# Setup of a graph-attention kernel: the q term in four column groups, the first mask counts in a step of their own, and the row flags read back half a batch later

## The chip, the core and the metric

The kernel runs on one core of a Trainium2 chip. The metric is the device time of one execution in microseconds, as the median of several. One execution was taken with the hardware profiler. Its views name the engines PE (matmul), PEld (weight load, beside PE), DVE (VectorE), ACT (ScalarE), POOL (GpSimd) and SP (the engine that issues most DMAs; "SPq" is its queue of issues).

## The reference, cut to what matters

```python
B, N, F = 16, 512, 512          # x; q is 16 x 512; the mask is 16 x 512 x 512 x 11 int32
H, dh, NONGT = 16, 32, 20       # heads, their width, keys per node
row_zero = x.sum(-1) == 0
q_exp = where(row_zero, 0, q[:, None, :])
self_feat = concat([x, q_exp]) @ W_self.T + b_self
output = self_feat
for d in range(2):              # the mask, and its transpose
    A = (mask if d == 0 else mask^T)[:, :, :20, :]
    cond, vb = A.sum(-1), A @ w_bias + b_bias
    qh = (self_feat @ Wq[d].T + bq[d]).reshape(B, N, H, dh)
    kh = (self_feat[:, :20] @ Wk[d].T + bk[d]).reshape(B, 20, H, dh)
    aff = where(cond > 0, einsum(qh, kh) / sqrt(dh), -9e15) + vb
    w = softmax(aff)
    output += einsum(einsum(w, self_feat[:, :20]), Wout[d]) + bout[d]
return x + relu(output)
```

All arithmetic is in float32.

## The kernel before, in words

**Setup, first part (lines 360 to 469).** The kernel first makes the self features of the 20 key nodes of all 16 batches (320 columns). SP issues the loads in the order of lines 379 to 400: the key columns `xkv` and the weights `ws_v` in three pieces, q as `q_sb`, the q half of the weights as `ws_q` (1 MB), then the key weights `wk`, `wq_sb`, the first x and mask tiles, and so on. PE multiplies `ws_v` with `xkv` into four PSUM banks `ps_kv` (L409). The q term is a product of its own: 16 matmuls `ps_q` (L424), each with a 128x128 block of `ws_q` as the weights and the 16 columns of `q_sb` as the moving operand. DVE copies the result to `qw` (L429). A matmul with a matrix of ones (`ps_nzk`, L434) sums x over the features, and DVE turns the sums into flags `nzk` (L435). DVE and POOL multiply flags and q term (`qp`, L442), DVE adds `ps_kv` (`kvn`, L446), ACT adds the bias (`kvT`, L449). PE then makes keys per direction and block (`ps_k`, L456), and ACT writes them to `khT` (L460).

**Setup, second part (lines 481 to 607).** The query weights are folded into the keys. Of 64 pieces PE makes three at a time, a burst: `keys(runs)` has four 32-row matmuls a piece (L534), two go to one pair of PSUM banks and two to a second pair. ACT copies the first pair to a staging tile `st` (L549), DVE the second (L551), and the next burst may overwrite a pair only after its copy. SP writes the tiles to DRAM (`g_d`, L554 to L558). There are 22 bursts, numbered n. Between two bursts the code puts other work, listed in `other`: the biases, the row flags of batches 0 and 1 (`row_flags`), the scores of the bias (`ps_c`, L487, four column groups of 32; their results go out through eight small DMAs that POOL issues, L494), the first self features (`ps_sf`, L186) and the values (`ps_v`, L507, whose results POOL writes out as `vw_d`, L517).

Three pieces of the main loop's work for batch 0 are put there by number: after burst 6 `mask_mul(0, 0)` and `mask_count(0, 0)`, after burst 8 `mask_add(0, 0)`, `load_cq(0)` and `row_sums(1)`, after burst 18 `full_add(0, 0)`. A mask half (256 nodes) passes through three steps. `mask_mul`: ACT casts the 880 integers to float (L207), POOL multiplies them with the bias weights (L208). `mask_count`: DVE counts the entries (L213) and turns the counts into 0 or -9e15 (L214). `mask_add`: DVE reduces the products (`lb`, L220), adds (L222), and ACT spreads the result (`both`, L227). `row_sums(1)` is three additions on POOL (`rx`, L163 and L165).

The order on each engine follows the program, but the scheduler moves some instructions of the main loop up: the count of mask half (0, 1) stands on DVE beside that of (0, 0), and the cast and product of (0, 1) stand on ACT and POOL within the bursts. The product tile `prod` has one buffer, so the second cast waits until the first product has been reduced (L220).

**Main loop.** For each of 16 batches there are four tiles nt of 128 nodes. A tile has the matmuls of the next self features (`ps_sf`, L186) and the scores (`ps_s`, L246), softmax on DVE, ACT and POOL, and once per batch the attention matmuls of the batch before (`ps_o`, L311) and the output. PE, DVE, ACT and POOL each keep an order of their own; SP issues in program order and waits at each issue for what that transfer needs. From batch 2 on the row flags take a way through DRAM: at nt 3 of batch b `row_mask(b + 2)` makes them on DVE and writes 2 KB to `nz_d` (L154), and right behind it `load_nz(b + 2)` reads them back to all partitions (L158). They are first used by `self_copy` (L199) at nt 3 of batch b + 1.

## Time and profile before

| | us |
|---|---|
| median of 3 runs (lowest, highest) | 644.77 (643.81, 644.95) |
| the profiled execution's own time | 644.1 |
| its span, first to last instruction | 642.2 |
| PE busy | 623.5 |
| DVE busy | 525.1 |
| POOL busy | 335.7 |
| ACT busy | 217.0 |

The profiled execution took 644.1 us in all, 0.7 us less than the median, of which 642.2 us lie between its first and last instruction. Busy times are sums over an engine's instructions. A wait "[2.93 <-DVE st L551]" behind a row means that the engine stood idle for 2.93 us before it, and that the copy at line 551 on DVE ended the wait. PEclk is the share of the full TensorE clock that was granted in a stretch.

### The profile page before, as it was taken

What the parts mean: (1) busy time and instruction counts of PE and PEld (TensorE: products, weight loads), DVE (VectorE), ACT (ScalarE), POOL (GpSimd) and SP (SyncE); (2) the same over time, 40 slices, a digit from 0 to 9 for tenths busy, and PEclk for the clock granted to TensorE, in tenths of its full rate; (3) what the DMA queues carried; (4) which work ended last, traced back from release to release, by engine and by line L of the source; (5) the groups of instructions that cost most, each with busy time, mean ns of one, the idle gap of its engine ahead of it and who ended that gap; (6) DMA issues with size and microseconds to landing.
All of it is one profiled execution on the core that took longest, in us unless ns stands there. A gap on an engine that the chain in (4) does not pass through costs nothing.

```text
span 642.2 us, 16385 instructions
## 1 busy us (share of the span) xinstructions
PE 623.5 (97%) x6830; PEld 373.7 (58%) x6830; DVE 525.1 (82%) x815; ACT 217.0 (34%) x479; POOL 335.7 (52%) x252
## 2 busy tenths in 40 slices
PE   8998999999999999999999999999999999999992
PEld 7654446655566565656565656565656565656552
DVE  0558554989898989899898989898989898989896
ACT  0334431415242424333242424252525151523232
POOL 1307121534738282837474747465565657474754
PEclk9898999999999999999999999999999999999997
DMA  8987899676546465656474646575746565644112
GB/s 289 397 331 248 344 370 342 174 230 213 199 154 222 156 213 157 204 165 222 147 234 146 224 153 231 154 242 155 242 154 227 169 211 186 209 122 145 66 67 100
DMA packets 89921, 131.87 MB, mean 205 GB/s; under 512 B 9240, under 2 KB 59960, under 8 KB 87800
## 3 DMA queue, kind: packets, MB, share of 16 engines
q1 hardware_dynamic: 89176, 129.47, 60.3%
q0 software_dynamic: 672, 1.36, 0.8%
q8 instruction: 54, 0.88, 0.6%
q14 instruction: 19, 0.16, 0.1%
HBM read 90.89 MB, written 39.92 MB: 204 GB/s over the span
## 4 chain that ended last, share of the span: by engine, by line
PE 84%; DVE 2%; ACT 1%; issue 0%; DVEq 0%; ACTq 0%
PE ps_s L246 43%; PE ps_sf L186 33%; PE ps_o L311 6%; PE ps_v L507 1%; ACT o L729 0%; PE ps_nz L169 0%; DVE s L284 0%; DVE mx L275 0%; DVE o L725 0%; DVE s L276 0%; PE ps_g(3, 0, 1, 1, 2)0_687 L534 0%; PE ps_g(3, 3, 0, 0, 2)0_764 L534 0%; PE ps_g(3, 2, 0, 1, 2)0_738 L534 0%; PE ps_g(3, 1, 1, 0, 2)0_710 L534 0%; DVE ps_s L273 0%
## 5 line engine op out<-in xcount | busy, mean ns | idle before, releaser
L246 PE MATMUL ps_s<-g,sf 128*64 128x320 f32 x2048 | 286.9, 433 | 0.0
L186 PE MATMUL ps_sf<-x,ws_v 128*64 128x256 f32 (+1 forms) x2048 | 221.4, 371 | 0.0
L246 PEld LDWEIGHTS ps_s<-g,sf 128*64 128x64 f32 x2048 | 145.8, 137 | 125.4 <-issue 6.2
L186 PEld LDWEIGHTS ps_sf<-x,ws_v 128*64 128x64 f32 x2048 | 146.7, 137 | 71.9 <-issue 1.7
L293 POOL TENSOR_TENSOR s<-s,sm 128x640 f32<-128x640 f32 x63 | 80.1, 1271 | 146.8 <-DVE sm L292 145.5
L266 ACT ACTIVATE s<-s 128x640 f32<-128x640 f32 x63 | 46.5, 738 | 239.8 <-DVE s L261 239.8
L236 POOL TENSOR_TENSOR full<-cq,both 128x640 f32<-128x640 f32 x64 | 99.1, 1548 | 27.0 <-ACT both L227 23.5
L208 POOL TENSOR_TENSOR prod<-prod,wb_sb 128x880 f32<-128x880 f32 x32 | 61.3, 1916 | 57.3 <-ACT prod L207 57.3
L257 DVE TENSOR_TENSOR ps_s<-ps_s,full 128x640 f32<-128x640 f32 x63 | 52.3, 830 | 42.5 <-PE ps_s L246 42.4
L333 POOL TENSOR_TENSOR o<-o,x 128x512 f32<-128x512 f32 x60 | 75.2, 1274 | 0.0
L227 ACT COPY both<-add 64x80 f32<-64x80 f32 x128 | 32.8, 256 | 76.1 <-DVE add L222 75.0
L291 DVE TENSOR_REDUCE sm<-s 128x32 f32<-128x640 f32 x63 | 51.7, 820 | 6.0 <-ACT s L266 0.9
L199 DVE SCALAR_TENSOR_TENSOR sf<-nz,qw,ps_sf 128x236 f32<-128x236 f32 (+1 forms) x128 | 52.6, 458 | 3.0 <-PE ps_sf L186 3.0
L259 DVE TENSOR_REDUCE mx<-ps_s 128x32 f32<-128x640 f32 x63 | 51.9, 824 | 2.2
L261 DVE TENSOR_TENSOR s<-ps_s,mx 128x640 f32<-128x640 f32 x63 | 51.9, 824 | 2.2
L300 DVE STREAM_TRANSPOSE wt<-s 128x640 f32<-128x640 f32 x63 | 52.5, 834 | 0.0
L311 PE MATMUL ps_o<-wt,vd 32*32 32x256 f32 (+2 forms) x2176 | 46.3, 374 | 6.3 <-issue 4.0
L330 ACT ACTIVATE o<-o,bo 128x512 f32<-128x512 f32 x60 | 40.0, 714 | 27.4 <-DVE o L324 25.0
L311 PEld LDWEIGHTS ps_o<-wt,vd 32*32 32x32 f32 x2176 | 31.0, 103 | 22.1 <-issue 14.6
L324 DVE TENSOR_TENSOR o<-ps_o,sf 128x512 f32<-128x512 f32 x60 | 36.3, 667 | 0.0
L213 DVE TENSOR_REDUCE cond<-adj 128x80 f32<-128x880 int32 x32 | 33.1, 1036 | 1.8 <-DMA adj<-in_adj 1.8
L149 ACT ACTIVATE xn<-xn 128x512 f32<-128x512 f32 x56 | 34.3, 614 | 0.0
(199 smaller groups left out, 440.5 us busy)
## 6 DMA issues: line engine op xcount, KB each, us to landing
g<-g_d SPq DMA_DIRECT2D x15, 1280.0 KB, 6.3
g_d<-st SPq DMA_DIRECT2D x16, 1120.0 KB, 5.5
x<-in_xT SPq DMA_DIRECT2D x16, 1024.0 KB, 9.3
out_T<-o SPq DMA_DIRECT2D x61, 256.0 KB, 2.0
xn<-in_xn SPq DMA_DIRECT2D x28, 512.0 KB, 6.6
adj<-in_adj SPq DMA_DIRECT2D x32, 440.0 KB, 8.6
vd<-bd_d SPq DMA_DIRECT2D x64, 128.0 KB, 2.6
nz<-nz_d SPq DMA_DIRECT2D x14, 256.0 KB, 4.0
```

The costliest lines, as they stand in the source:

```text
L186: nc.tensor.matmul(held[0][bass.ts(a, R), i * N // 2 : i * N // 2 + hi - lo], ws_v[:, k, bass.ds((2 * f + i) * P + a * R, R)], xs[b][:, k, ...
L199: nc.vector.scalar_tensor_tensor(sfs[b][:, 2 * f + i, lo:hi], nzs[b][:, lo:hi], qw[:, 2 * f + i, b : b + 1], ps[:, i * N // 2 : i * N // 2 ...
L208: nc.gpsimd.tensor_mul(p, p, wb_sb.unsqueeze(1).to_broadcast([P, 2 * S, L]))
L236: nc.gpsimd.tensor_add(f, cqs[b].unsqueeze(1).to_broadcast(shape), adds[b, nt // 2][:, nt % 2].unsqueeze(2).to_broadcast(shape),)
L246: nc.tensor.matmul(ps[bass.ts(a, R), g, : W // 2], sfs[b][:, k, bass.ds(nt * P + g * R, R)], keys[:, k, a], start=(k == 0), stop=(k == C - 1),
L257: nc.vector.tensor_add(pw, pw, fulls.pop((b, nt)).rearrange("p g h m -> p g (h m)"))
L259: nc.vector.tensor_reduce(mx, p4, AX.X, ALU.max)
L261: nc.vector.tensor_sub(s, p4, mx.unsqueeze(3).to_broadcast(full))
L293: nc.gpsimd.tensor_mul(s, s, sm.unsqueeze(3).to_broadcast(full))
L300: nc.vector.transpose(wts[b][:, nt], s.rearrange("p a h m -> p (a h m)"))
L311: nc.tensor.matmul(banks[q][bass.ts(e, DH)].rearrange("p (t n) -> p t n", n=32), vds[b][r, e, i, q // 2 * 2 + n], wt[r, :, bass.ts(j, 32)] ...
L333: nc.gpsimd.tensor_add(o[:, c], o[:, c], xs[b][:, c])
```

## The change: what it does

**The q term.** `q_sb` becomes four blocks of 32 columns, of which 16 hold q and 16 are set to zero by DVE. Instead of 16 matmuls there are four, one for each block of 128 inputs: the weights are the 32 columns of `q_sb`, the moving operand is a 512-column row of `ws_q`, and each writes a column group of its own of one PSUM bank. ACT copies this bank to `q4`. Four further matmuls with a 0/1 matrix `sel` (128x16) sum the four groups and turn the result to the layout of before. POOL makes `sel` at the start with a memset and four `affine_select` instructions. The four last matmuls and the copy to `qw` come between the products of column blocks 2 and 3. The sums for the flags go to the second bank of the same PSUM tile.

**The first masks.** `mask_count(0, 0)` stays after burst 6, `mask_mul(0, 0)` moves to after burst 7, `mask_add(0, 0)` and `load_cq(0)` to after burst 9, `row_sums(1)` to after burst 11. A mask tile is no longer removed from its table when it is counted.

**The row flags.** `load_nz(b + 1)` is issued at nt 1 of batch b behind `load_cq(b + 1)`, half a batch after the write.

```diff
-        a = adjs.pop((b, h))
+        a = adjs[b, h]
...
-        q_sb = sp.tile([P, C, B], F32, name="q_sb")
+        q_sb = sp.tile([P, C, DH], F32, name="q_sb")
+        sel = sp.tile([P, B], F32, name="sel")
...
             nc.vector.memset(ones, 1.0)
+            nc.vector.memset(q_sb[:, :, B:], 0.0)
             nc.vector.memset(bqbd, 0.0)
             nc.gpsimd.memset(zero, 0.0)
+            nc.gpsimd.memset(sel, 0.0)
+            for k in range(C):
+                nc.gpsimd.affine_select(
+                    out=sel, in_=sel, pattern=[[-1, B]], compare_op=ALU.not_equal, fill=1.0,
+                    base=-k * DH, channel_multiplier=1,
+                )
...
-            rows(q_sb, qT)
+            rows(q_sb[:, :, :B], qT)
...
-            ps = ps_s.tile([P, 2, 512], F32, tag="s", name="ps_q")
-            for fc in range(C):
-                for i in range(C):
-                    nc.tensor.matmul(
-                        ps[:, fc % 2, fc // 2 * B : (fc // 2 + 1) * B],
-                        ws_q[:, i, bass.ts(fc, P)], q_sb[:, i],
-                        start=(i == 0), stop=(i == C - 1),
-                    )
-            nc.vector.tensor_copy(qw..., ps...)
-            ps = ps_s.tile([P, 2, 512], F32, tag="s", name="ps_nzk")
-            nc.tensor.matmul(ps[:, 0, :BM], ones, rsk, start=True, stop=True)
-            nc.vector.tensor_scalar(nzk, ps[:, 0, :BM], 0.0, None, ALU.not_equal)
+            ps = ps_s.tile([P, 2, 512], F32, tag="s", name="ps_q4")
+            for k in range(C):
+                nc.tensor.matmul(ps[bass.ts(k, DH), 0], q_sb[:, k], ws_q[:, k], start=True, stop=True)
+            q4 = sk.tile([P, F], F32, name="q4")
+            nc.scalar.copy(q4, ps[:, 0])
+            nc.tensor.matmul(ps[:, 1, :BM], ones, rsk, start=True, stop=True)
+            nc.vector.tensor_scalar(nzk, ps[:, 1, :BM], 0.0, None, ALU.not_equal)
             for fc in range(2, C):
                 for k in range(2, C):
                     kv_terms(fc, k)
+                if fc == 2:
+                    ps = ps_s.tile([P, 2, 512], F32, tag="s", name="ps_q")
+                    for c in range(C):
+                        nc.tensor.matmul(
+                            ps[:, c % 2, c // 2 * B : (c // 2 + 1) * B], q4[:, bass.ts(c, P)], sel,
+                            start=True, stop=True,
+                        )
+                    nc.vector.tensor_copy(qw..., ps...)
...
                 if n == 6:
+                    mask_count(0, 0)
+                if n == 7:
                     mask_mul(0, 0)
-                    mask_count(0, 0)
-                if n == 8:
+                if n == 9:
                     mask_add(0, 0)
                     load_cq(0)
+                if n == 11:
                     row_sums(1)
...
                         load_cq(b + 1)
+                        if b > 0:
+                            load_nz(b + 1)
...
-                    if nt == 3:
-                        load_nz(b + 2)
```

More of the change, by code (lines that the diff above doesn't have):

```diff
@@ L419, in gat_kernel @@
                     kv_terms(fc, k)
-            ps = ps_s.tile([P, 2, 512], F32, tag="s", name="ps_q")
-            for fc in range(C):
-                for i in range(C):
-                    nc.tensor.matmul(
-                        ps[:, fc % 2, fc // 2 * B : (fc // 2 + 1) * B],
-                        ws_q[:, i, bass.ts(fc, P)], q_sb[:, i],
-                        start=(i == 0), stop=(i == C - 1),
-                    )
-            nc.vector.tensor_copy(
-                qw.rearrange("p (i a) b -> p a i b", a=2),
-                ps[:, :, : 2 * B].rearrange("p a (i b) -> p a i b", b=B),
-            )
-            ps = ps_s.tile([P, 2, 512], F32, tag="s", name="ps_nzk")
-            nc.tensor.matmul(ps[:, 0, :BM], ones, rsk, start=True, stop=True)
-            nc.vector.tensor_scalar(nzk, ps[:, 0, :BM], 0.0, None, ALU.not_equal)
+            ps = ps_s.tile([P, 2, 512], F32, tag="s", name="ps_q4")
[5 more added lines that the diff above has]
+            nc.vector.tensor_scalar(nzk, ps[:, 1, :BM], 0.0, None, ALU.not_equal)
             for fc in range(2, C):
@@ L438, in gat_kernel @@
                     kv_terms(fc, k)
+                if fc == 2:
[5 more added lines that the diff above has]
+                        )
+                    nc.vector.tensor_copy(
+                        qw.rearrange("p (i a) b -> p a i b", a=2),
+                        ps[:, :, : 2 * B].rearrange("p a (i b) -> p a i b", b=B),
+                    )
             for fc in range(C):
```

## The prediction

> **What bounds the kernel now.** I read the chain that ended last first.

> ```profile
> span 642.2 us, 16385 instructions
> ...
> PE 623.5 (97%) x6830; PEld 373.7 (58%) x6830; DVE 525.1 (82%) x815; ACT 217.0 (34%) x479; POOL 335.7 (52%) x252
> ...
> PE 84%; DVE 2%; ACT 1%; issue 0%; DVEq 0%; ACTq 0%
> ```

> 84% of the chain is matmul work. The parts of the change that lie in the main loop therefore gain only where PE stands idle. The waits of PE, longest first, say where:

> ```profile
> PE ps_o L311 <- issue: 4.0, 2, 2.8
> PE ps_g(1, 2, 0, 0, 2)1_489 L534 <- DVE st L551: 2.9, 1, 2.9
> PE ps_o L311 <- DVE wt L285: 2.3, 1, 2.3
> PE ps_warm L370 <- DVE ones L365: 1.1, 1, 1.1
> PE ps_q L424 <- DMA ws_q<-in_wsT: 0.9, 1, 0.9
> ```

> Of the first row 2.8 us and all of the third lie in the tail, which is not touched; 1.19 us lie in the first attention, at 146. The second row is the large one. The timeline around it:

> ```profile
> 54.26 3.77 DVE L214 TENSOR_SCALAR cond<-cond 128x80 f32<-128x80 f32 x2
> 54.83 1.92 POOL L208 TENSOR_TENSOR prod<-prod,wb_sb 128x880 f32<-128x880 f32 x1
> 55.57 0.81 PE L534 MATMUL ps_g(1, 2, 0, 0, 2)0_488<-khT,wq_sb 32*128 32x320 f32 x4
> 56.70 1.27 POOL L163 TENSOR_TENSOR rx<-x 128x512 f32<-128x512 f32 x1
> 57.96 1.21 DVE L551 TENSOR_SCALAR st<-ps_g(1, 1, 0, 1, 2)1_462 128x320 f32<-128x320 f32 x2
> ...
> 59.31 0.54 PE L534 MATMUL ps_g(1, 2, 0, 0, 2)1_489<-khT,wq_sb 32*128 32x320 f32 x2 [2.93 <-DVE st L551]
> ```

> Two instructions on 80 numbers hold DVE for 3.77 us. Their row alone shows 2.562 and 1.291 us; the shortest of all 32 of this line takes 0.201. The first ends at 56.82 and the second at 58.03, each as an instruction of POOL ends. The copy behind them is late, and PE waits for the bank. The clock then falls (columns: stretch, length, busy time with counts of PE, PEld, DVE, ACT, POOL, granted clock, DMA share, GB/s):

> ```profile
> 13.10:16.50 3.40, 3.40 (x31) 3.40 (x32) 0.00 (x0) 1.28 (x1) 0.00 (x0) 1.00 1.05 397
> 16.60:19.90 3.30, 3.30 (x8) 2.22 (x8) 1.85 (x5) 0.21 (x1) 1.20 (x2) 0.50 1.06 401
> ...
> 56.40:59.30 2.90, 0.00 (x0) 0.02 (x1) 2.90 (x5) 0.00 (x0) 2.82 (x3) 1.00 0.67 255
> 59.30:60.90 1.60, 1.59 (x14) 1.10 (x15) 1.02 (x3) 0.66 (x2) 1.27 (x2) 1.00 0.19 58
> 61.00:64.20 3.20, 3.20 (x16) 1.18 (x18) 1.98 (x4) 1.73 (x5) 0.48 (x1) 0.50 1.00 371
> ```

> It is at 0.50 after the stall, and also from 16.6 to 19.9, behind 3.4 us of the 16-column matmuls `ps_q`.

> **The change part by part. Masks.** Between the end of the `ps_sf` matmuls at 55.57 and the end of burst 11 (the start of `ps_v` at 70.38) PE takes 14.8 us. Later bursts without a wait take 1.03 (72.29 to 73.32), a group of `ps_v` 1.91 with four records and 1.18 with two: four bursts and their groups would take 9.1, so 5.7 us are lost: 3.7 in the stalled burst, 1.6 in the two slow rows at half clock, 0.4 later.

> In the changed order `mask_mul(0, 0)` comes behind burst 7's copies on ACT. The cast (0.94) then starts when these end, POOL's product 55.9 instead of 54.83. In times of before: the two counts end at 54.35. POOL issues the eight `cq_d` transfers until 54.81. If these issues hold DVE as the product does, the L214 pair ends at 55.2 (two of 0.20 behind 54.81), 0.7 before the product; if they do not, at 54.8. The copy L551 (1.21) ends at 56.4 instead of 59.17. PE wants that bank some 0.4 after 55.57. Burst 6, whose second pair came 0.71 late, took 1.72; here it comes 0.9 late, so I take 1.95 for burst 8, a loss of 0.9.

> A new wait stands in place of the old one. `lb` (L220, 1.06) and L222 (0.30 here) now follow the copies of burst 9 on DVE, and on ACT the cast of mask half (0, 1), which waits for `lb`, and the four `both` copies stand before the copy of burst 10. In times of before: burst 8 ends at 57.5, `ps_v` 59.4, burst 9 60.5, copies on DVE to 61.8, `lb` to 62.9; cast 0.93, `both` 1.05, copy 1.03 on ACT to 65.9. PE comes to burst 11 at 57.5 + 1.91 + 1.03 + 1.18 + 1.36 (a burst with a slightly late pair, as at 83.31) + 1.91 = 64.9. It waits 1.0 and ends the burst at 66.9 instead of 70.4. **Masks: -3.5** (to -5.4 if neither wait shows, to 0 if the pair is still held).

> `row_sums(1)` takes 3.9 us of POOL behind `vw_d`'s first issue; its reader at 93.39 has over 20 us of cover, and the `vw_d` issues behind it are wanted at 116.5. `load_cq(0)` moves past three SP issues (about 1.6 us); its reader is at 94.57. Both cost 0; without that cover they would cost at most 3.9 and 1.6.

> **q.** Removed: 16 matmuls, 3.77 us. Added: four with 512 columns. The nearest row is `ps_c`, also four column groups: eight matmuls of 320 columns take 1.28 us, which serial at 2 x 0.267 each would be 4.3. Scaled to four of 512: 1.0 (serial 3.4). From 13.05, when `ws_q` lands as before, they end at 14.05. The matmul for the flags now writes the same PSUM tile that ACT copies to `q4`, and in the changed program it waits for ACT: copy of 128x512 about 0.7 (ACT rows of that width: 0.61 to 0.71), so PE is idle to 14.9; queued behind it are all PE's next products. Flags 0.55, column block 2 1.07, four `sel` matmuls 0.92 (eight records of 0.115 as in `ps_q`), to 17.45. `qw` ends at 17.8, and DVE's row `qp` starts there instead of 18.64; `nzk` is out of its way. The 3.8 us from it to the last `kvT` stay, so PE's `ps_k` gains 0.8. Key weights are there: SP's issue at 23.93 ended a wait for `wq_sb`, needed at 25.35 after the shift. The table load on ACT waits for nothing now and moves to the start.

> Against that stands the clock. **Row:** a stretch with 1.6 us of work in some 3.4 (the idle stretch and the one behind it) was followed by half clock; the first attention, with 1.19 idle in 3.4, was not (1.00 after it). So the limit lies between 47% and 65%. [...] By the row, the 3.4 us from 16.5 hold about 1.7 of streaming (column block 3 1.07, 0.5 of `ps_k`, 0.1 of `sel`), 50%, near the row that was throttled. Half clock over `ps_k` eats the 0.8, and 0.8 more if it falls where PE doesn't wait for `kvT` anyway. The row decides on the masks. For q I take **-0.4**, halfway between warm and cold, since 50% lies inside the open interval; ends -0.8 and +0.8.

> On POOL, `sel`'s memset and four `affine_select` precede the sums `rsk`. No row shows them; memsets are 0.1 to 0.2, a 128x320 addition 0.86. POOL is idle from 0.93 to 4.88, and `rsk` (ends 9.08) is wanted at 14.9: 9.8 us of cover. I take 0. Bounds: nothing, and what passes 9.8. DVE's memset of `q_sb` (nearest, 0.27) is done long before the load.

> **Row flags.** `load_nz` leaves the place where SP waited for the 2 KB write (7.5 us in its first three). Behind it stood stores and `xn` loads, for which no engine on the chain waits. At its new place it adds one issue of 0.33 behind `cq`, with nothing to wait for. In batch 2 `cq` is issued by 172.0, the first use is at 193.9 (127.23 plus two batches of 33.35): 22 us for a landing of 3.7 to 4.9. **0.** Bounds: 1.2 gained if the first attention's wait went, 1.0 lost if the earlier `xn` load slowed the mask tile that DVE waits for at 136.75 (the 2 KB write behind that tile landed with it, so transfers do not overtake, and I take nothing).

> A second cost has no cover to spare: with the stall gone, bursts follow at 2.94 us throughout, where DMA share was 0.94. A late last `g_d` would move what follows; up to 1, in the range.

> **Sum.** -3.5 - 0.4 = -3.9 on the profiled execution, whose own time is 644.1 (span 642.2 and 1.9 around): 640.2. The median lies 0.67 above it, so **640.9**.

> **The rivals.**
> - More goes (0.16): clock warm, the ACT wait hidden, perhaps the first attention's wait gone too. -3.5 - 1.0 - 0.8 - (0 to 1.2): 638.3 to 639.5, say 638.6. For it: 0.5 to 1 us decide. Against: ACT's order has no gap there.
> - Part of it is given back through DMA or cold q (0.10): 642.3.
> - The change doesn't do what it says (0.08): L214 is still held, because the pair isn't through before POOL's product starts. It is held to that product's end, PE waits nearly 3 us again, and only about 0.8 remains: 644.0. It decides where DVE is 0.7 later than worked out.
> - Slower (0.04): `affine_select` is long. It delays `rsk`, and PE's queue behind the flags. It decides over 9.8 + 3.9 = 13.7 us for the four, 3.4 each; at 5 each, 10.2 late, 651.1. Against: 16 columns, and all other POOL rows.
> - The forecast itself: 0.62, 639.9 to 641.9.

> **How the numbers follow.** 0.2%, 1.3 us, is about what a measurement of this kernel can tell from no change. Faster: 0.62 + 0.16 + 0.10 = 0.88; same 0.08; slower 0.04. The range 638.5 to 643.0 leaves out the last two cases and about half of the first rival, 0.2 in all.

> **What would show it.** L214 near 0.2 to 0.8 each and before the product; PE's 2.9 us wait gone, and a wait of about 1 at burst 11 on ACT's copy; no half clock near 61; four `ps_q4` in 1.0 and PE idle 0.8 behind them; `ps_k` 0.4 to 0.8 earlier; from burst 11 on everything 3.9 earlier. It is wrong if PE still waits for L551 near 56, if `rsk` ends after 14, or if the main loop gains or loses by batch.

## The result, and the profile after

| | before | after |
|---|---|---|
| median of 4 runs, us (lowest, highest) | 644.29 (642.81, 644.95) | 638.66 (638.31, 639.12) |
| the profiled execution's own time | 644.1 | 639.12 |
| its span | 642.2 | 637.0 |

The medians are 5.6 us apart, where 3.9 less had been forecast. The ratio is 0.989 (95% interval 0.9861 to 0.9919); the two medians alone make 0.991. The direction is right, the size is not: the forecast ratio, 640.9 / 644.77 = 0.994, lies outside the interval. The median is only just within the forecast range of 638.5 to 643.0, and the ratio, taken of the 644.77 that the forecast started from, makes 637.7, which is below it.

PE's busy time fell from 623.5 to 618.3, although no matmul of the main loop is gone:

```profile
PE 618.3 (97%) x6814; PEld 368.8 (58%) x6814; DVE 521.6 (82%) x816; ACT 217.5 (34%) x480; POOL 336.6 (53%) x257
```

Of PE's waits, the 2.9 us on L551's copy is gone. A shorter one on ACT's copy at burst 11 stands in its place, and in q's part there are new ones, on the copy of q and on `kvT`:

```profile
PE ps_k L469 <- ACT kvT L462: 1.1, 2, 0.8
...
PE ps_g(2, 0, 0, 1, 2)0_570 L547 <- ACT st L562: 0.9, 1, 0.9
PE ps_q L435 <- ACT q L434: 0.8, 1, 0.8
```

The timeline of the same place. The first three rows answer to the prediction's third block, the others are the chain that the prediction foresaw (`lb`, cast, `both`, copy, burst 11):

```profile
48.23 5.14 POOL L507 DMA_DIRECT2D cq_d<-c  x8 [17.52 <-ACT c L505]
52.82 0.32 DVE L214 TENSOR_SCALAR cond<-cond 128x80 f32<-128x80 f32 x2
54.42 1.91 POOL L208 TENSOR_TENSOR prod<-prod,wb_sb 128x880 f32<-128x880 f32 x1 [1.04 <-ACT prod L207]
...
59.66 1.06 DVE L220 TENSOR_REDUCE lb<-prod 128x80 f32<-128x880 f32 x1
60.76 0.93 ACT L207 CAST prod<-adj 128x880 f32<-128x880 int32 x1 [1.26 <-DVE lb L220]
61.59 1.06 ACT L227 COPY both<-add 64x80 f32<-64x80 f32 x4
62.67 1.03 ACT L562 ACTIVATE st<-ps_g(1, 3, 1, 0, 2)0_546 128x640 f32<-128x640 f32 x2
63.76 0.41 PE L547 MATMUL ps_g(2, 0, 0, 1, 2)0_570<-khT,wq_sb 32*128 32x160 f32 x2 [0.87 <-ACT st L562]
```

The two counts took 0.32 us together instead of 3.77, and they ran while POOL was still issuing the `cq_d` transfers (48.23 to 53.37). So these issues did not hold DVE here.

The granted clock in the stretches that the prediction showed, the first of the last three columns being the clock:

```profile
16.60:19.90 3.30, 2.51 (x12) 1.47 (x11) 2.70 (x7) 1.12 (x2) 1.76 (x2) 1.00 1.06 402
56.40:59.30 2.90, 2.90 (x21) 1.06 (x19) 1.19 (x4) 0.83 (x2) 0.00 (x0) 1.00 1.02 403
61.00:64.20 3.20, 2.33 (x14) 1.03 (x18) 1.83 (x4) 2.64 (x7) 2.44 (x2) 1.00 0.97 359
```

Both half-clock stretches are gone (0.50 and 0.50 before), and PE works through 56.40 to 59.30, where it had stood idle.

Four marks divide the span of every kernel that ran, and the table says where each gained. Column A is when `ws_q` has landed and q's matmuls start. B runs from there to the first `ps_g`. C runs from the first `ps_sf` of the set-up to the first `ps_sf` of its second group (at 94.44 in before), and so holds bursts 8 to 11; that mark lies 4.20 us ahead of the main loop's first `ps_sf` in every profile. D is what the first attention loses: batches (not half-batches, as one of the expectations below has it) follow each other every 33.345 us, and D is by how much the second group of `ps_o` comes later than 84.52 (51.17 + 33.345) behind the end of C. From the first `ps_g` to the first `ps_sf` every profile has 25.57 to 25.59. From the second group of `ps_o` to the end every profile but one has 461.4 to 461.5 (own product buffer 462.6), so A to D hold nearly all that differs. The kernels are explained below; all is in us, the last column is the median over all runs of that row, and rows of different groups ran on different chips.

| kernel | A | B | C | D | span | median |
|---|---|---|---|---|---|---|
| before | 13.05 | 12.43 | 43.38 | 1.76 | 642.2 | 644.29 |
| before, once more | 13.11 | 14.09 | 44.61 | 2.27 | 645.6 | 647.59 (one run) |
| after | 12.47 | 11.57 | 39.32 | 2.10 | 637.0 | 638.66 |
| after, once more | 12.74 | 11.58 | 39.31 | 4.45 | 639.6 | 638.97 |
| masks alone | 13.09 | 12.70 | 39.31 | 1.64 | 638.3 | 640.36 |
| q alone | 11.98 | 11.57 | 44.45 | 4.44 | 644.0 | 644.32 |
| flags alone | 12.98 | 12.43 | 43.37 | 1.99 | 642.3 | 646.05 |
| row sums alone | 12.28 | 14.10 | 42.29 | 1.68 | 641.9 | 644.24 |
| product alone | 12.38 | 11.69 | 41.34 | 2.62 | 639.6 | 640.83 |
| own bank | 12.43 | 10.75 | 39.31 | 1.62 | 635.6 | 638.30 |
| own product buffer | 11.91 | 11.58 | 38.83 | 2.97 | 638.0 | 638.53 |
| mask first | 12.21 | 11.58 | 39.31 | 0.00 | 634.6 | 636.90 |
| bank + mask first | 12.23 | 10.75 | 39.31 | 0.00 | 633.8 | 636.18 |
| all three | 12.44 | 10.74 | 38.82 | 1.04 | 634.6 | 635.74 |

Before to after, in the two first profiles: A -0.58, B -0.86, C -4.06, D +0.34, together -5.16 of the 5.2 us.

### The profile page after: what moved, and what is told of

It is laid out like the page before. It is cut to its first block, busy times and chain, and to the rows that moved or that the text cites. A ratio compares the mean times of both kernels' runs of the same rounds, so it can differ in the third digit from the quotient of the medians.

```text
span 637.0 us, 16366 instructions
## 1 busy us (share of the span) xinstructions
PE 618.3 (97%) x6814; PEld 368.8 (58%) x6814; DVE 521.6 (82%) x816; ACT 217.5 (34%) x480; POOL 336.6 (53%) x257
## 3 DMA queue, kind: packets, MB, share of 16 engines
q0 software_dynamic: 672, 1.36, 0.9%
## 4 chain that ended last, share of the span: by engine, by line
PE 84%; DVE 2%; ACT 1%; issue 0%; DVEq 0%; ACTq 0%
PE ps_s L246 43%; PE ps_sf L186 33%; PE ps_o L311 6%; PE ps_v L520 1%; ACT o L744 0%; PE ps_nz L169 0%; DVE s L284 0%; DVE mx L275 0%; DVE o L740 0%; DVE s L276 0%; PE ps_g(3, 3, 0, 0, 2)0_773 L547 0%; PE ps_g(3, 2, 0, 1, 2)0_747 L547 0%; PE ps_g(3, 1, 1, 0, 2)0_719 L547 0%; PE ps_g(3, 0, 1, 1, 2)0_696 L547 0%; DVE ps_s L273 0%
## 5 line engine op out<-in xcount | busy, mean ns | idle before, releaser
L208 POOL TENSOR_TENSOR prod<-prod,wb_sb 128x880 f32<-128x880 f32 x32 | 61.3, 1916 | 61.4 <-ACT prod L207 61.4
L311 PE MATMUL ps_o<-wt,vd 32*32 32x256 f32 (+2 forms) x2176 | 46.4, 375 | 6.7 <-issue 4.4
L311 PEld LDWEIGHTS ps_o<-wt,vd 32*32 32x32 f32 x2176 | 31.2, 104 | 22.4 <-issue 14.9
```

Source lines behind the costliest of these rows:

```text
L208: nc.gpsimd.tensor_mul(p, p, wb_sb.unsqueeze(1).to_broadcast([P, 2 * S, L]))
L311: nc.tensor.matmul(banks[q][bass.ts(e, DH)].rearrange("p (t n) -> p t n", n=32), vds[b][r, e, i, q // 2 * 2 + n], wt[r, :, bass.ts(j, 32)] ...
```

## The experiments

Each ratio is to the kernel before, run on the same chip beside the group (medians 645.67 for the first four, 645.47 for the kernel after and the three single edits on it, 646.02 for the product alone and the combinations).

### The parts one by one

**Masks alone:** the kernel before with this part of the change (and the mask tile kept in its table).

```diff
                 if n == 6:
-                    mask_mul(0, 0)
                     mask_count(0, 0)
-                if n == 8:
+                if n == 7:
+                    mask_mul(0, 0)
+                if n == 9:
                     mask_add(0, 0)
                     load_cq(0)
+                if n == 11:
                     row_sums(1)
```

> The kernel before with the mask part alone (count of block 0 behind burst 7, product behind burst 8, second mask's sums behind burst 11); q and the flags as before. Theory A (no DVE count is held any longer, GpSimd's DMA issues hold nothing, and bursts 8 to 11 lose what they lost in the kernel after): from the end of ps_sf to ps_v 10.7 to 10.9 us instead of 14.8, so -4.1 there, of which the first attention's wait gives back 0.2 to 0.4: 3.7 to 4.0 us under before, ratio 0.994. Theory B (as the prediction had it, the issues of cq_d hold a count to 53.4 and burst 8 takes 1.95): -3.5. The clock falls to 0.50 near 16.6 as before, because q is as before.

Measured: ratio 0.9926 (0.9901 to 0.9951), C 39.31 against 43.38, so -4.07, as theory A has it. The pair of counts took 0.32 us. The clock still fell at 16.3 and came back at 19.7.

**q alone:** the kernel before with the four column groups, `sel` and the copy to `q4`, as in the diff of the change.

> The kernel before with the q part alone (four column groups, selection matmuls). Theory A (the 64 thin matmuls pulled the clock down, the four wide ones do not): first ps_g 0.86 after the load of ws_q is taken out, full clock from 16 to 20; -0.8 to -0.9 us. Theory B (half of it, as the prediction had it): -0.4. Theory C: ws_q also lands 0.6 earlier because of this part; then -1.4 in all, and ws_q's landing near 12.47 here, near 13.05 in the runs with q as before. If the landing varies from run to run without regard to the kernel, it is no part of the change.

Measured: ratio 0.9985 (0.9962 to 1.0008), which settles nothing by itself. The profile does: B is 11.57, as in the kernel after, so theory A holds for the stage. The gain was lost twice later. C was 44.45, 1.07 worse than in the first profile of before, with half clock from 56.2 to 63.1 instead of 61.0 to 64.4. And the first attention waited 2.54 us and was then put on half clock as well (these windows, and those below, are 3.41 us long for a reason that follows):

```profile
144.98:148.39 3.41, 0.87 (x39) 0.39 (x34) 3.34 (x7) 1.02 (x4) 1.34 (x2) 1.00 0.23 82
148.39:151.80 3.41, 3.41 (x112) 2.15 (x89) 3.23 (x5) 1.43 (x4) 1.48 (x1) 0.50 0.02 5
```

`ws_q` landed at 11.98 here, but at 12.28 and 12.38 in two kernels with q as before (the next experiments) and at 12.74 in a run of the kernel after. The two groups overlap, so theory C is not shown.

**Flags alone:** the kernel before with `load_nz` moved, as in the diff of the change.

> The kernel before with the flag part alone (row flags read half a batch later). Theory: nothing, within 0.2 us; SP's wait of 6 us for the flags' write is gone from before x's load, but nothing on the way to the end waited for that load; the first attention's wait stays at 1.2. Rival: the loads queued behind it come earlier and the first attention's wait shrinks by up to 1.2.

Measured: ratio 1.0014 (0.9989 to 1.0039), A to C within 0.1 us of before, first attention's wait 1.42. SP no longer stands 5.5 us behind the flags' write (131.4 to 136.9 in before), and no gain shows.

**Row sums alone:** the kernel before with one call moved.

```diff
                 if n == 8:
                     mask_add(0, 0)
                     load_cq(0)
+                if n == 11:
                     row_sums(1)
```

> The kernel before with one call moved: the second mask's row sums go from behind burst 8 to behind burst 11; the count, its order against the product and all else stay. Theory A (what costs is the pair of counts held under GpSimd's work, and the clock's fall near 61 is its consequence): the first count is still held to about 56.8, the second is free, PE's wait falls from 2.9 to about 1.9 and the clock stays full, about -2.5 us. Theory B (the clock falls all the same): about -1.1 us. Theory C (the count that comes first is simply held for longer): no change.

Measured: ratio 0.9973 (0.9944 to 1.0003). The first count is held as before, the second runs as soon as the product is done:

```profile
55.16 2.69 DVE L214 TENSOR_SCALAR cond<-cond 128x80 f32<-128x80 f32 x2
55.74 1.93 POOL L208 TENSOR_TENSOR prod<-prod,wb_sb 128x880 f32<-128x880 f32 x1
```

PE's wait fell to 1.8, but the clock still fell (59.5 to 62.9). C is 42.29: 1.09 less, theory B. B was 14.10, although nothing there is edited.

**Product alone:** the kernel before with the other call moved (and the mask tile kept in its table).

```diff
                 if n == 6:
-                    mask_mul(0, 0)
                     mask_count(0, 0)
+                if n == 7:
+                    mask_mul(0, 0)
                 if n == 8:
                     mask_add(0, 0)
```

> The kernel before with one other call moved: the first mask's product on GpSimd goes from behind burst 6's place to behind burst 7's, so that both counts stand ahead of it; the row sums of the second batch and the mask's addition stay where they were. Theory A (an elementwise operation of GpSimd holds a VectorE count that starts beside it to its end, its DMA issues do not): both counts take 0.3 together as in the kernel after, ps_sf to ps_v falls from 9.26 to about 6, -3 to -4 us. Theory B (the row sums hold the counts too, wherever the product is): the second count still takes 1.3, ps_sf to ps_v about 7 to 8. Theory C (VectorE now waits for the product at the mask's addition, with burst evictions behind it): a new wait of 1 to 2 us at burst 8 or 9 takes half of it back.

Measured: ratio 0.9918 (0.9888 to 0.9948). The two counts take 0.32 together, and from `ps_sf` to `ps_v` it takes 5.80 as in the kernel after, so theory A holds up to there. C, however, is 41.34, only 2.04 less than before: theory C holds behind it. POOL's row sums now hold another short instruction of DVE, L222 (1.17 us), and the burst that waits for what follows is late:

```profile
56.32 1.26 POOL L163 TENSOR_TENSOR rx<-x 128x512 f32<-128x512 f32 x1
...
57.65 2.61 POOL L165 TENSOR_TENSOR rx<-rx,x 128x512 f32<-128x512 f32 x2
57.85 1.17 DVE L222 SCALAR_TENSOR_TENSOR add<-cond,bb_sb,lb 128x80 f32<-128x80 f32 x1
...
61.22 0.54 PE L534 MATMUL ps_g(1, 3, 1, 0, 2)0_541<-khT,wq_sb 32*128 32x320 f32 x2 [1.71 <-ACT st L549]
```

L222 takes 0.30 in the kernel after. It ended here at 59.02; the `rx` addition that began at 57.65 ends at 58.92. Not every DVE instruction was held: the reduction L220 at 56.75 takes 1.06 beside the first `rx` addition, as in the kernel after, and in before the two copies L551 out of PSUM take their usual 1.21 beside the second (57.96 and 58.04). Half clock from 61.8 to 65.2 followed.

In stage C of these profiles the two moves bring -1.09 and -2.04 alone and -4.07 together. What is missing in the sum is at least in part the half clock that each of them still has; where its windows fall differs from one execution to the next, and these are one profile each. The timed runs do not tell the product alone (0.9918) from the masks' part as a whole (0.9926), so that the gain needs both moves is read from C and not shown by the times.

### The clock

B was 11.7, 12.4, 12.7 and 14.1 in kernels with the same instructions there. So the kernel before ran once more.

> The kernel before once more, for one profile. Theory (the clock is settled every 3.41 us on a grid that falls anew in each execution): the grid differs from the first profile's, and with it the number of half-clock stretches, each 3.4 or 6.8 us long: q to ps_g is 11.7 with none, 12.4 to 12.7 with one, about 14 with two; ps_sf to the main loop is 43.4 to 44.5 with one or two. VectorE's two held counts (2.56 and 1.29) and TensorE's wait of 2.9 repeat to 0.1. ws_q lands anywhere from 12.0 to 13.1. Rival: the stages repeat the first profile to 0.1 us, the half-clock stretches begin at the same instruction, and the differences between the kernels with q as before are their edits' doing.

Measured: B 14.09 and C 44.61 with the very same kernel, 3.4 us more span than in its first profile, while the two counts (3.80 together) and PE's wait for L551 (2.95) repeat to 0.1 us. So the differences in B between kernels with the old q need no edit to explain them. The windows (columns as in the prediction) show why:

```profile
12.46:15.87 3.41, 2.76 (x25) 2.79 (x25) 0.00 (x0) 1.28 (x1) 0.00 (x0) 1.00 1.05 403
15.87:19.28 3.41, 3.41 (x13) 2.82 (x13) 0.60 (x2) 0.00 (x0) 0.00 (x0) 0.50 1.06 393
19.28:22.69 3.41, 3.41 (x8) 2.23 (x7) 2.65 (x6) 1.58 (x3) 1.76 (x2) 0.50 1.05 409
```

In the six profiles whose changes of clock are read to 0.1 us or better (before and after twice each, q alone, product alone) the half-clock stretches ahead of the tail are 3.4 or 6.8 us long, and within a profile the changes lie whole multiples of 3.413 us from each other: in the first profile of before the stretches begin at 16.58, 60.95 and 634.39, the later ones 13 and 181 times 3.413 behind the first; in the second at 15.84, 60.21 and 633.65, again 13 and 181. From the one execution to the other the grid lies 0.74 us elsewhere. Of the windows at full clock with a wait in them, those of the 16-column matmuls left aside, a busy share of 0.25 at 145.0 (q alone) and of 0.27 at 140.1 (after, once more) was followed by half clock, shares of 0.55 and more in the two first profiles were not. In between it went either way (0.47 in the tail of before and 0.50 in the first attention of its second profile were not, 0.48 at 57.5 in before and 0.50 at 58.5 with the product alone were). The 16-column matmuls fill the window with their records: behind 3.4 us of them (13.2 to 16.6 in before, all busy) came half clock, and so it did in the second profile of before, with 0.80 of the window ahead taken by them. B was 12.43 to 14.10 in five of the six profiles with the old q. In the sixth (product alone) the grid cut this stretch in two, 0.49 and 0.58 of two windows, the clock stayed at 1.00, and B was 11.69.

### The changed kernel, and three edits on it

The kernel after ran again beside them. The intervals of the three edits all overlap with its own, so what each does is read from the stages of one profile each.

> The changed kernel as it is, on the chip of the three runs that alter it. Theory (the clock is settled every 3.41 us by how busy TensorE was in the 3.41 us before): the times of its stages repeat the first profile to 0.1 us from the landing of ws_q to the first attention (q to ps_g 11.57, ps_g to ps_sf 25.58, ps_sf to ps_v 5.80), wherever the grid of 3.41 us falls, as no stretch of 3.41 us there is less than half busy; only the landing of ws_q (12.0 to 13.1) and the first attention's wait (1.1 to 2.5) move. Rival: ps_sf to ps_v or q to ps_g differ by 1 us or more from run to run, and the first profile was a lucky one.

Measured: ratio 0.9901 (0.9876 to 0.9927), A to C as expected to 0.01 us but for the landing. Of the 2.6 us by which the span differs between its two profiles, 0.27 is the landing and 2.35 the first attention, which this time waited 2.56 and was on half clock from 143.4 to 146.9.

**Own bank:** the flags' sums go to a PSUM tile of their own.

```diff
-            nc.tensor.matmul(ps[:, 1, :BM], ones, rsk, start=True, stop=True)
-            nc.vector.tensor_scalar(nzk, ps[:, 1, :BM], 0.0, None, ALU.not_equal)
+            pz = ps_s.tile([P, 2, 512], F32, tag="s", name="ps_nzk")
+            nc.tensor.matmul(pz[:, 0, :BM], ones, rsk, start=True, stop=True)
+            nc.vector.tensor_scalar(nzk, pz[:, 0, :BM], 0.0, None, ALU.not_equal)
```

> The changed kernel with a PSUM tile of its own for the flags' matmul, which so no longer waits behind ScalarE's copy of q. Theory A (the 0.8 us of idle TensorE ahead of the flags' matmul lies on the path): q to ps_g 10.8 instead of 11.57, -0.8 us. Theory B (the wait moves: qw's copy or kvT's eviction comes no earlier, and ps_k's waits on ScalarE grow by as much): q to ps_g 11.2 to 11.6, -0.0 to -0.3 us.

Measured: ratio 0.9889 (0.9863 to 0.9915) to before, B 10.75, so -0.83 in the stage: theory A. The flags' matmul follows without a gap:

```profile
12.43 1.07 PE L432 MATMUL ps_q<-ws_q,q_sb 128*32 128x512 f32 x8 [0.55 <-DMA ws_q<-in_wsT]
13.43 0.81 PE L436 MATMUL ps_nzk<-rsk,ones 128*128 128x320 f32 x2
```

**Own product buffer:** the first product lies in a load tile, so the second cast has nothing to wait for.

```diff
-        p = prods[b, h] = msk.tile([P, 2 * S, L], F32, tag="prod", name=f"prod{b}_{h}", bufs=1)
+        if (b, h) == (0, 0):
+            t = load.tile([P, 2, F], F32, tag="xn", name="prod0_0").rearrange("p j f -> p (j f)")
+            p = prods[b, h] = t[:, : 2 * S * L].rearrange("p (m l) -> p m l", l=L)
+        else:
+            p = prods[b, h] = msk.tile([P, 2 * S, L], F32, tag="prod", name=f"prod{b}_{h}", bufs=1)
```

> The changed kernel with a buffer of its own for the first mask's product, so that the second mask's cast on ScalarE does not wait for the reduction of the first product. Theory A (ScalarE's late start on 'both' and on the eviction of burst 10 is what TensorE waits for at burst 11): the 0.9 us wait at burst 11 is gone or under 0.3, ps_sf to ps_v 5.1 instead of 5.80, -0.7 to -0.9 us. Theory B (the chain is product, reduction, 'both' on ScalarE, and the cast was in nobody's way): the wait stays at 0.8 to 0.9, no change.

Measured: ratio 0.9892 (0.9868 to 0.9916). The wait at burst 11 fell from 0.9 to 0.4 and C to 38.83: -0.48, between the theories. `ps_sf` to `ps_v` stayed at 5.80; the 5.1 expected there was wrong, since burst 11 comes behind the first `ps_v`. The profile also has a wait of 1.92 ahead of the last 13 matmuls that no other profile shows.

**Mask first:** the next mask is loaded ahead of the megabyte of x.

```diff
-                    if b + 2 < B:
-                        load_x(b + 2)
                     if b + 1 < B:
                         load_adj(b + 1, 1)
+                    if b + 2 < B:
+                        load_x(b + 2)
```

> The changed kernel with the load of the next mask issued ahead of the 1 MB load of x for two batches on. Theory A (the first attention waits because the mask lands behind that megabyte): VectorE's wait for the mask at 131.6 goes (2.2 to 0), TensorE's 1.5 us at 140.7 goes, -1.2 to -1.5 us; the later batches, which do not wait there, stay as they are. Theory B (x comes 1.7 us later and something waits for it): under -0.5 us, and a wait for x appears on POOL's or TensorE's queue. The wait's size varied from 1.1 to 2.5 over the profiles so far.

Measured: ratio 0.9869 (0.9843 to 0.9895), D 0.00: theory A, and more than its 1.5. The wait's row understates the loss, since it counts from the end of the six matmuls ahead of it as the profile shows it (0.63 us behind the first): the seventh matmul of this attention begins 2.17 us behind the first in the kernel after and 0.04 behind it here, and the difference is D to 0.03 us. The mask's count runs at 129.05 instead of 131.60, where DVE had waited 2.21 us for the mask. In the kernel after, the count's second instruction, L214, is moreover held again by POOL's product:

```profile
132.71 1.93 DVE L214 TENSOR_SCALAR cond<-cond 128x80 f32<-128x80 f32 x1
132.66 1.91 POOL L208 TENSOR_TENSOR prod<-prod,wb_sb 128x880 f32<-128x880 f32 x1 [1.85 <-ACT prod L207]
```

and with the mask loaded first:

```profile
123.85 0.42 SPq L93 DMA_DIRECT2D adj<-in_adj  x1
...
129.05 1.01 DVE L213 TENSOR_REDUCE cond<-adj 128x80 f32<-128x880 int32 x1
130.09 0.51 DVE L214 TENSOR_SCALAR cond<-cond 128x80 f32<-128x80 f32 x1
```

L214 takes 1.93 at this place in the kernel after and 1.92 in before, where DVE waited 2.21 and 1.85 us for the mask, and 0.51 here, so the late mask cost DVE its lateness and 1.4 us more.

**Two and three edits together:**

> The changed kernel with two of the edits: own PSUM tile for the flags' matmul, mask ahead of x; the products share their buffer as in the changed kernel. Sum of the traces: -0.82 and -2.10, so -2.9 us against the changed kernel, about 636; burst 11 keeps its wait of 0.9, the tail has no wait for the last matmuls. q to ps_g 10.75, ps_sf to ps_v 5.80, first attention 33.35 behind the start of batch 0's second half. Rival: with TensorE earlier by 0.8 the mask is late again, a wait of up to 0.8 comes back and it is -2.1.

> The changed kernel with the three edits together: own PSUM tile for the flags' matmul, own buffer for the first product, mask ahead of x. If they add up as their traces say (-0.82 from q to ps_g, -0.48 in bursts 8 to 11, first attention's loss of 2.10 against a full half-batch of 33.35 to 0): -3.4 us against the changed kernel, about 635.5. If the wait of 1.9 us for the last 13 matmuls, which the profile with the product's own buffer showed and no other, belongs to that edit: -2.2 us and the same wait here.

Measured: with two edits 636.18 us, ratio 0.9846 (0.9815 to 0.9876); with all three 635.74, ratio 0.9838 (0.9807 to 0.9869). Two add up as expected (B 10.75, D 0.00). The third brings its 0.49 in C, but D was 1.04: SP issued the mask at 125.10 instead of 122.98, DVE waited 0.55 us for it, and L214 took 1.93 instead of 0.52, so the late mask was back. In both profiles with the own product buffer SP issued the `vd` loads ahead of it later behind C (34.9 and 35.8 us) than in the other twelve (33.4 to 34.4); whether that edit does it is not shown. The intervals of the two versions overlap, so that the third edit adds anything is not shown either. The wait in the tail did not come back in this profile; what it was stays open. All runs of both versions were faster (634.9 to 637.0) than all runs of the kernel after (638.3 to 641.5), though on another chip.

## Why the forecast was right in its direction and too small

Three terms of the sum were off by about half a microsecond each in the two first profiles: the masks (0.56 more than forecast), q (0.46 more) and the landing of `ws_q` (0.58, not forecast); the first attention took 0.34 of it back. That makes 5.16 for 3.9. The rest of the way from 640.9 to 638.66 lies mostly in the step from one profile to the median.

**The masks' mechanism held.** Each step came as worked out: the counts through before the product, PE's 2.9 us wait and the half clock near 61 gone, `lb`, cast, `both` and copy in a chain on ACT, a wait of 0.87 at burst 11 (1.0 forecast). The mis-sized term is burst 8. The prediction took 1.95 us, because it let the `cq_d` issues hold the counts as the product does. Burst 8 took 1.29 (54.13 to 55.42), and the counts took 0.32 beside the issues. That term is 0.66 of the sum; masks were -4.06 instead of -3.5.

**The q term failed at the clock.** The work itself was right: eight records in 1.06 (1.0 forecast), a copy of 0.59 (0.7), an idle 0.79 behind it (0.9). But without half clock the old order takes 11.69 and the new one 11.57, so the work gains 0.1. What the part gains is mostly the clock: 0.74 of the 0.86 in the two first profiles, and up to 2.4 of 2.5 against the other profiles. The prediction counted the half clock from 16.6 to 19.9 as given, asked whether the *new* order might be too thin, and put -0.4 halfway. Its warm end, -0.8, was what came. It had also laid the windows of the new order where they lay in the one profile of before. In the eight profiles with the new q, B was 11.57 or 11.58, and 10.74 or 10.75 with the own bank, and the clock, where it was read there (kernel after, bank + mask first, all three), was 1.00. That the fall came behind the 16-column matmuls (0.50 from 16.58 on) stood in its own rows ("behind 3.4 us of the 16-column matmuls"), but the sum did not use it. `ps_k` began 1.57 us earlier relative to the load, more than the 0.4 to 0.8 forecast, and that behind a wait of 0.79 for `kvT`; its fifth record then began 1.68 us behind the first instead of 1.08, again for `kvT`, and so 0.86 was left at `ps_g`.

**One profile was taken for the kernel.** This step failed too: the sum was made against an execution with one half-clock window at q and one at burst 8, and 0.67 us was added for the median. The kernel after has its median 0.46 below its profiled execution, so this term alone was off by 1.13 of the 2.24 us between forecast and result. Old q over six profiles is B 12.91 on average (11.69 to 14.10), old masks over four (before twice, q alone, flags alone) C 43.95. Against 11.57 and 39.31 that is -1.3 and -4.6, 6.0 together, less what the first attention gives back. That is the size of the 5.6 and 6.5 us between the medians on the two occasions, but no exact account of them. The highest of 29 timed runs of before took 651.56; the two profiles do not explain that one.

**First attention:** forecast 0, with a bound of 1.0 lost; it was 0.34 worse in the first pair of profiles, as the mask came in only 5.15 earlier while PE came 5.5 earlier. Its size varies between executions of the same kernel (2.10 and 4.45), so how much of it is the change's isn't settled. **The landing of `ws_q`,** 0.58 earlier, was not forecast. Its average is 12.8 in six profiles with the old q and 12.3 in eight with the new one, and the groups overlap; whether the change moves it stays open.

**Flags 0, POOL's extra work 0:** as forecast. The four `affine_select` took 1.00 us together at 1.05.

**The rivals.** "More goes" came nearest (638.6 for 638.66), but the match is luck: of its three means only the full clock came, the wait on ACT was not hidden and the first attention's wait did not go. L214 was not held, and the rivals on the other side did not occur.

## What to carry to other kernels

A stall's price was not its length here. The clock changed in steps of 3.413 us. Half clock came behind a window that a wait had left half empty (busy share 0.48 at 57.5 in before) and behind 3.4 us of 16-column matmuls, and a half-clock window cost another 0.7 to 1.3 us (B 12.43 with one and 14.09 with two, against 11.69 with none; in the first attention of the kernel after D 4.45 against 2.10, of which the longer wait is 1.02). Whether it came depended on where the windows fell in that execution. When part of an edit's gain is clock, take two or three profiles of the kernel before and compare stage by stage between fixed marks. In a kernel like this one, short instructions on DVE like L214 and L222 are worth keeping clear of POOL's elementwise work: beside the product L214 took 2.56 us, beside the row sums L214 took 1.29 and L222 1.17, where 0.20 and 0.30 are their shortest times in before. The reduction L220 (1.06) and the two copies out of PSUM (1.21) were not held.
